# Two linear-attention layers on one core: norm scalars on GpSimd, sequence marks made once, a new instruction order

## The chip, the cores and the metric

The kernel runs on one core of a Trainium2 chip. The metric is the device time in microseconds (us) of one execution. A core has five engines with an in-order queue each: TensorE (PE; its weight loads are listed as PEld), VectorE (DVE), ScalarE (ACT), GpSimd (POOL) and SyncE (SP), which here issues all DMA transfers.

## What is computed

Input x has 32 sequences of 128 tokens with 512 features, all in float32. Two layers of the same build follow each other (layer 0 with 16 heads, layer 1 with 8). Cut to what matters, a layer is:

```
xn = layernorm(x) * w + b
q, k, v = xn @ Wq + bq, xn @ Wk + bk, xn @ Wv + bv      # 512 x 512 each
k, v masked at padded tokens
q = softmax(q over the features of a head); k = softmax(k over the tokens)
att = k^T v per head;  y = q att
scale, shift = split(silu(cond) @ We + be)              # cond: 32 x 1024
h = silu(layernorm(y) * (1 + scale) + shift) @ Wo + bo
x = x + h
```

In layer 0 the mask sets k to minus infinity. A sequence whose tokens are all masked therefore gives NaN in the reference, and the kernel carries this as a mark per sequence (`nanf`: 0, or NaN for a fully masked one) which is added to the residual stream in layer 1.

## The kernel before

**Jobs.** A job is two sequences (G = 2) of one layer; there are 16 jobs per layer, 32 in all, in one row. Tiles have 128 partitions. Per job: the rows of x are loaded (`z`), normalized, transposed to `xnT`, and multiplied with the weights. Products with the weights are done by a seven-product scheme (sums of blocks, `Sx` and `Sh`, made on GpSimd; sums of weights made once), in which each product lands in one of the PSUM banks `qa`, `qb`, `qc`, `qe`, `ka` and so on, and VectorE or ScalarE adds it to its destination (`kadd`, `qadd`, `oadd`). In the middle jobs (`far`) transposes are done by VectorE in 32x32 blocks plus DMA through DRAM (`zb`/`zd`, `k`/`kd`, `yb`/`yd`, and `qb` to `qT`); the first and the last job use PE transposes.

**Norm scalars.** `norm` takes the statistics of 512 features by `bn_stats` and `bn_aggr` on VectorE (`mv`: mean and variance), adds epsilon on VectorE (L570), raises to the power of -1/2 on GpSimd (L571, `rstd`), and makes -mean * rstd on VectorE (L573, `nmr`) for both sequences at once. ScalarE then normalizes with `nmr` as bias and `rstd` as scale (L585). The first and the last job (`apart`, also called edge) normalize on VectorE with mean and `rstd` directly (L581). There are two norms per job: "a" of x and "b" of y.

**Marks and residual.** In layer 0 every job makes the marks of its two sequences from its mask (L605 to L608: maximum over the masked row, comparison, reciprocal, product with zero), and GpSimd adds the output bias row to the residual tile `x` (L619). In layer 1 VectorE adds bias row and mark at once (L622). Then `oadd` adds the output products in quarters of 128x256 (L918), and the tile is stored.

**Order.** Nothing runs in program order. Every step is registered with `op(place, engine, cost, ...)` with a due time: the job's start (31 us per job) plus a due time written in the code plus a shift from the table `SHIFT[place]`. `Plan.schedule` then places the steps one by one by modelled costs, hops between engines (`HOP`, `SAFE`), buffers that come free, and due times. The emitted list fixes the order of each of the five queues, SP with its DMA issues among them. `lock=True` makes the planner keep VectorE and GpSimd steps apart. Before, the table has three stages: preparation, layer 0 and layer 1.

Of the kernel before, what the change touches and what calls it, by code (L numbers as in the profile page):

```python
# [38 lines left out]
    0: ([-3.7, -3.3, 10.9, -8.6, -4.2, 13.5, 4.9, 11.2, -18.2, 15.7], [-33.7, 9.7, -1.7, 28.5, -9.3], [14.4, 7.7]),  # L39
    1: ([], [-26.7], []),  # L40
    2: ([], [11.5], []),
    3: ([], [-31.7], []),
    4: ([], [-5.4], []),
    5: ([-16.7, -7, -12.1, -13.1, -3.6, -5.6, -16.5, -9.3, 22.1, -11.3, -17.4, 10.8], [], [-15.8, -20.2, 3.4, -3.6, -4.7, 13.7, 27, 5.9, 15.4, 2.5, -8.5, -11.3]),
    6: ([], [31.1, 22.7, 25.5, 1.5, 21.3, 20.6, -5.4, 18.5, 30.4, 28.7, 24.3, 22.4], [19.8, 18.9, 12.7, 41.8, 17.6, 19.7, 11.5, 33.5, 23, 31.2, 30.4, 14.8]),
    7: ([-32.7, -45.9, -34.3, -37.3], [-21, -27.4, -89.5, -25.3], [-16, -29.6, -16.3, -153.3]),
    8: ([-20.6, -23.4, 25.4, -50.1], [-20.3, -46.7, -5.3, -20.8], []),
    9: ([-33.4, -50.5], [-0.6, -8.9], []),
    10: ([16.7], [14.1], []),
    11: ([4.2], [48.6], []),  # L50
    12: ([5], [1.3], []),
    13: ([-18.6], [-4.2], []),
    14: ([-10], [14.9], []),
    15: ([19.1], [20.7], []),
    16: ([6.1], [], []),
    17: ([], [-103.2, -62, -106.9, -143.3, -159.3, -84.2, -88.8, -123.6], [-126, -130.5, -80.2, -30.5, 41.4, -77.8, -45.7, -9.4]),
    18: ([], [13.4, -27.4, -24.8], [-19.4, 46, -28.9]),
    19: ([], [-65.7, -82.4, -54.5, -91.8, -71.3, -58.9, -72.7, -62.7, -4.4, -61.3, -71.7, 1.2], [-88.4, -41.6, -56.9, -56.8, -67.7, -22.8, -22.6, -73.8, -126.4, -37.7, -117.1, -19]),
    20: ([], [49.4, 1.5, 71.9, 14.9], [77.1, -16.1, 62.3, -1.5]),
    21: ([], [58.9, 65, 31, 76.4], [78.7, 91.3, 57.5, 72.3]),  # L60
    22: ([], [66.3, -8, 5.7, -6.5], [-7.3, 50.9, 0.8, -8.9]),
    23: ([], [-23.5, 26.7, 58.4, 48.5], [-1.3, 58.3, 47.2, 35.9]),
    24: ([], [71.8, 1.1], [2.7, 30.5]),
    25: ([], [-16.9, -35.1, 13.9, -9.1], [5.1, 4.6, -17.3, -2.1]),
    26: ([], [65.9, 92.9, 20.2, -15], [1.2, 49.1, 24, 91.5]),
    27: ([], [-1.8], []),
    28: ([], [36.7], []),
    29: ([], [-70.3], []),
    30: ([], [-13.2], []),
    31: ([], [4.6], []),  # L70
    32: ([], [], [17]),
    33: ([], [-70.6, -36.8], []),
    34: ([], [], [20.7, 30]),
    35: ([], [-2.2, 52.4], [29.7, 43.1]),
    36: ([], [60.7, 29.9, 17.5, 35.6], [-22.4, -40.6, 16.5, 9.8]),
    37: ([], [0.9, -44.2], [-21.1, -40.5]),
    38: ([], [85.9, -9, 10.6, -29.4], [14.5, -6.6, 8.9, -45.6]),
    39: ([], [-50.7, -15, -36.2, -35.4, -53.2, -20, -62.5], [-45.9, -38.8, -4, 5.6, -15.3, -23.9, -141]),
    40: ([], [11.9, 18.7, 39.5, -35.9, -20.5, -34.5, 16.3, -33.4], [-27.7, -28.4, -11.5, -45.7, 20.4, -36.9, 6.6, -64.2]),
    41: ([], [-54.2, -47.2, -6.3, -19.6], [28.2, 8.8, -55.8, 21.1]),  # L80
    42: ([], [-47.8, -30.7, -46.4, -22.4], []),
    43: ([], [-24.9, -43, 11.6, 31.4], []),
    44: ([], [-54.4, -66.3], [-38.9, 25.9]),
    45: ([], [19.9, -42.6], [0.2, 2.4]),
    46: ([], [65.6, 73.3, 119, 122.5, 87.6, 49.7, 33.8, 82.8], [154.5, 165.3, 80, 165.8, 68, 49.2, 148.7, 120.9]),
    47: ([], [5.2, 0.8], [14.1, 37.1]),
    48: ([], [59.3, -10.4], []),
    49: ([], [-31.3, -4, -17.3, -29.4, -31.9, -35.8, -34.7], [-8, -9.4, -26.2, -33.6, -77.1, 5.2, -12.3]),
    50: ([], [-223, -129.1, -153.9, -150.7], [-149.5, -120.6, -102.4, -178.6]),
    51: ([], [-66.1, -38.1, -35, -81.1], [-64.5, -158.5, -51.3, -23]),  # L90
    52: ([], [-2.6, 1.4, 2.4, 16.2], []),
    53: ([], [5.4, -14.2, -29.9, -9.3], []),
    54: ([], [4.1, 24.4], [63.9, -18.5]),
    55: ([], [-51.7, -23.9], [-47.5, -89.4]),
    56: ([], [62.1, 69.2], [49.3, -25.6]),
    57: ([], [-18.1, -40.7], [-106.3, -28]),
    58: ([], [75.4, -28.7], [-7.9, -18.2]),
    59: ([], [83.4, 26.3], [29.1, 34.8]),
    60: ([], [55.2, 48.7, 115, 61, 38.4, 30, 73.5, 87, 1.5, -15.2, 72.4, -21.6, 21.2, 79.6, 85.8, 7.1], [45.5, 99.4, 58.5, 121.8, 14.6, 53.3, 3.3, 83.5, 17.6, 83.6, 152.4, 57.6, 10.2, 100, 99.7, 82.6]),
    61: ([], [53.1, 61.3], [45.3, 77.6]),  # L100
    62: ([], [-7.6, 11.1], [-3.7, 21.5]),
    63: ([], [-11.9, 26.1], [-9, 17.1]),
    64: ([], [76.4, 89.5], [85.6, 75.2]),
    65: ([], [-11, -1.1], [-16.2, 13]),
    66: ([], [], [21.8, -4.9]),
# [200 lines left out]
def act(n, pointers=0, psum=True):  # L306
    return (0.05 if psum else 0.093) + 0.093 * pointers + n / 1200
# [705 lines left out]
```

## Time and profile before

| what | us |
|---|---|
| runs shown, without profile | 932.77, 942.49, 942.39 (median 942.39) |
| the profiled execution, own time | 935.26 |
| its span, first to last instruction | 933.5 |
| PE busy | 906.3 (97%), 6292 matmuls |
| VectorE busy | 838.9 (90%) |
| ScalarE busy | 595.8 (64%) |
| GpSimd busy | 452.5 (48%) |
| DMA moved | 183.38 MB, mean 196 GB/s |
| granted TensorE clock, mean | 0.998 |

Busy times are unions of an engine's instructions. Ends of matmuls are modelled, so a busy PE is not PE at its peak; the distance of one row's start to the next tells more. The share of an engine is a mean over stages: the start, in which weights are loaded, the middle, in which two to three jobs overlap, and the end, in which the last job runs alone. A stage's idle time is its length less the busy time there. Groups of instructions are listed as: line, engine, operation, written tile <- read tiles, shape, count | busy us, mean ns of one | idle time before them, and what ended it.

### The profile page before, as it was taken

The page shows a single profiled execution, that of the slowest core. Times are in us where ns is not written, and L with a number is a line of the kernel's source. Part 1 is how long each engine was busy: PE and PEld are TensorE (multiplying, and loading weights), DVE is VectorE, ACT ScalarE, POOL GpSimd, SP SyncE. Part 2 cuts the span into 40 slices and gives each one's busy share as a digit, 9 for nine tenths or more (in the row PEclk, how much of TensorE's full clock was granted, in tenths as well). Part 3 has the DMA queues.
Part 4 walks back from the last instruction along what each step waited for, and adds up shares of the span by engine and source line. Part 5 has one row for each costly group of instructions (what it writes and reads, how often), then busy time and mean ns, then how long its engine had stood idle before and what let it go on. Part 6 is the DMA issues. An engine that isn't in the chain of part 4 may idle for free.

```text
span 933.5 us, 18771 instructions
## 1 busy us (share of the span) xinstructions
PE 906.3 (97%) x6292; PEld 637.8 (68%) x6292; DVE 838.9 (90%) x1844; ACT 595.8 (64%) x1503; POOL 452.5 (48%) x520
## 2 busy tenths in 40 slices
PE   6989999999999999999999999999999999999996
PEld 4546776676667667767766766777776767677675
DVE  5897989988789899799999999999989999888995
ACT  5447666585664957658577656766766756655652
POOL 3544475456554656556546344543444434343322
PEclk9999999999999999999999999999999999999999
DMA  9565568787676785778958876676767675655533
GB/s 324 179 195 156 163 186 229 206 259 206 189 211 201 188 237 156 204 225 236 274 165 226 229 230 169 184 220 187 196 203 214 209 202 144 172 158 140 155 121 109
DMA packets 239360, 183.38 MB, mean 196 GB/s; under 512 B 143136, under 2 KB 196896, under 8 KB 239264
## 3 DMA queue, kind: packets, MB, share of 16 engines
q1 hardware_dynamic: 239264, 182.18, 67.0%
q8 instruction: 50, 0.82, 0.4%
q14 instruction: 46, 0.38, 0.1%
HBM read 102.94 MB, written 63.44 MB: 178 GB/s over the span
## 4 chain that ended last, share of the span: by engine, by line
PE 55%; DVE 27%; DMA 7%; ACT 4%; SPq 4%; issue 2%; POOL 1%; ACTq 0%; DVEq 0%
PE bank_qa L739 10%; PE bank_qe L739 7%; PE bank_ka L665 5%; PE bank_oa L913 5%; PE bank_oe L913 4%; PE bank_qb L739 3%; PE bank_ke L665 3%; PE bank_py L868 3%; PE bank_qc L739 3%; DVE x L918 2%; PE bank_pa L847 2%; DMA yb<-yd 2%; PE bank_kb L665 2%; SPq L797 2%; PE bank_oc L913 2%
## 5 line engine op out<-in xcount | busy, mean ns | idle before, releaser
L710 POOL TENSOR_TENSOR kT<-kT,mb 128x512 f32<-128x512 f32 x64 | 82.7, 1297 | 107.3 <-DVE kT L676 80.8
L671 ACT ACTIVATE kT<-bank_ka,cols_c 128x128 f32<-128x128 f32 x248 | 75.2, 360 | 82.4 <-PE bank_ka L665 68.0
L717 ACT ACTIVATE kT<-kT,kmax 128x128 f32<-128x128 f32 x256 | 99.5, 390 | 37.4 <-DVE kmax L713 36.9
L739 PE MATMUL bank_qa<-wqv,Sx 128*128 128x512 f32 x248 | 117.5, 596 | 3.2 <-DVE v L743 2.0
L739 PE MATMUL bank_qe<-wqv,Sx 128*128 128x512 f32 x248 | 117.6, 596 | 1.7 <-DVE v L746 1.3
L899 ACT ACTIVATE hT<-yb,fc_c,fa_c 128x128 f32<-128x128 f32 x240 | 96.4, 481 | 9.2 <-DVE rstdb L570 8.8
L780 POOL TENSOR_TENSOR q<-q,qmax 128x512 f32<-128x512 f32 x64 | 67.6, 1065 | 62.1 <-DVE qmax L779 60.5
L544 POOL TENSOR_TENSOR Sx<-xnT 128x256 f32<-128x256 f32 x62 | 44.7, 737 | 98.8 <-PE bank_qe L739 71.0
L633 ACT ACTIVATE xnT<-zb,cols_c 128x256 f32<-128x256 f32 x116 | 60.8, 588 | 31.9 <-DMA zb<-zd 22.9
L585 ACT ACTIVATE y<-y,nmrb,rstdb 128x512 f32<-128x512 f32 x60 | 46.0, 805 | 44.8 <-DVE nmrb L573 44.7
L665 PEld LDWEIGHTS bank_ka<-Sx,wk 128*128 128x128 f32 x496 | 63.9, 192 | 15.2 <-issue 13.0
L739 PEld LDWEIGHTS bank_qe<-wqv,Sx 128*128 128x128 f32 x248 | 44.2, 190 | 41.2 <-issue 36.1
L665 PEld LDWEIGHTS bank_ke<-Sx,wk 128*128 128x128 f32 x496 | 62.9, 192 | 13.8 <-issue 9.3
L544 POOL TENSOR_TENSOR Sh<-hT 128x256 f32<-128x256 f32 x64 | 45.8, 728 | 52.7 <-ACT hT L899 50.0
L739 PEld LDWEIGHTS bank_qa<-wqv,Sx 128*128 128x128 f32 x248 | 43.7, 190 | 39.6 <-issue 33.6
L913 PE MATMUL bank_oa<-wo,Sh 128*128 128x256 f32 x256 | 66.6, 384 | 0.6 <-DVE x L918 0.2
L868 PEld LDWEIGHTS bank_py<-att_c,qT 128*128 128x128 f32 x512 | 61.1, 192 | 8.5 <-issue 4.3
L913 PE MATMUL bank_oe<-wo,Sh 128*128 128x256 f32 x256 | 65.8, 381 | 0.6 <-DVE x L918 0.5
L665 PE MATMUL bank_ke<-Sx,wk 128*128 128x128 f32 x496 | 65.7, 275 | 0.7 <-DVE kT L676 0.7
L665 PE MATMUL bank_ka<-Sx,wk 128*128 128x128 f32 x496 | 65.6, 275 | 0.0
L868 PE MATMUL bank_py<-att_c,qT 128*128 128x128 f32 x512 | 63.4, 276 | 2.0 <-DMA z<-in_x_dram 0.9
L585 ACT ACTIVATE z<-z,nmra,rstda 128x512 f32<-128x512 f32 x60 | 46.1, 805 | 28.8 <-DVE nmra L573 27.7
(126 smaller groups left out, 2225.6 us busy)
## 6 DMA issues: line engine op xcount, KB each, us to landing
x<-x SPq DMA_DIRECT2D x64, 256.0 KB, 3.7
kd<-k SPq DMA_DIRECT2D x30, 512.0 KB, 4.1
k<-kd SPq DMA_DIRECT2D x120, 128.0 KB, 3.2
qT<-qb SPq DMA_DIRECT2D x480, 32.0 KB, 2.3
yd<-yb SPq DMA_DIRECT2D x30, 512.0 KB, 3.5
yb<-yd SPq DMA_DIRECT2D x120, 128.0 KB, 3.4
zd<-zb SPq DMA_DIRECT2D x29, 512.0 KB, 3.2
zb<-zd SPq DMA_DIRECT2D x116, 128.0 KB, 3.4
```

What stands on the lines that cost most here:

```text
L544: op(17, "POOL", pool(2 * T), lambda i=i, x=x, y=y, f=f: nc.gpsimd.tensor_tensor(S.ap[:, i], x(), y(), f), r, [(S, i)], due=due, lock=True)
L585: op(26, "ACT", act(512, 2, False), lambda: nc.scalar.activation(dst.ap[:, b, :], src.ap[:, b, :], AF.Identity, bias=nmr.ap[:, b : b + 1], ...
L633: op(36, "ACT", act(GT, 2, False), lambda c=c: nc.scalar.activation(xnT.ap[:, c, :].rearrange("p (b r t) -> p r b t", b=G, r=4), zb.ap[:, ...
L665: nc.tensor.matmul(t.ap[:, m * T : (m + 1) * T], kw[quarter].ap[:, c, m * P : (m + 1) * P], a()[:, c, :], start=(first and m == 0 and c == ...
L671: op(40, "ACT", act(T, 1), lambda m=m: nc.scalar.activation(kT.ap[:, 2 * h + m, i, :], Ak.ap[:, m * T : (m + 1) * T], AF.Identity, bias=co ...
L710: op(44, "POOL", pool(2 * GT), lambda hs_=hs_: nc.gpsimd.tensor_tensor(kT.ap[:, hs_].rearrange("p m b t -> p m (b t)"), kT.ap[:, hs_].rear ...
L717: op(46, "ACT", act(T, 1, False) + 0.093, lambda m=m, b=b: nc.scalar.activation(kT.ap[:, m, b, :], kT.ap[:, m, b, :], AF.Exp, bias=km.ap[: ...
L739: nc.tensor.matmul(t.ap, a()[:, c, :], wqv[quarter].ap[:, c, :], start=(first and c == 0), stop=(c == 1), skip_group_check=not first)
L780: op(55, "POOL", pool(512, False), lambda qh=qh, qm=qm: nc.gpsimd.tensor_tensor(qh(), qh(), qm.ap[:, :H].unsqueeze(2).to_broadcast([P, H, ...
L868: nc.tensor.matmul(py.ap[:, m * P : (m + 1) * P], qTc(b, m), att.ap[:, b, m, :], start=True, stop=True)
L899: op(75, "ACT", act(T, 2, False), lambda c=c, b=b: nc.scalar.activation(hT.ap[:, c, b * T : (b + 1) * T].rearrange("p (r t) -> p r t", r=4 ...
L913: nc.tensor.matmul(t.ap[:, :hf], a()[:, c, :], ow[quarter].ap[:, c, :], start=(first and c == 0), stop=(c == 1), skip_group_check=not first)
```

## The change

- The epsilon add moves from VectorE to GpSimd, and so does the negated mean, which becomes two GpSimd instructions of one column each. A norm's scalars are then four GpSimd instructions in the middle jobs, in the first and last job two per sequence.
- The marks of all 32 sequences are made once: the transposed mask (128 tokens x 32 sequences) is loaded, turned into 0 or -1 by VectorE, summed over the tokens by a PE product with a tile of ones, and put through reciprocal and product with zero. The four VectorE instructions per job of layer 0 are gone.
- In layer 1 GpSimd now adds the bias row as in layer 0, and the mark is added with the first product of each output quarter (four of the eight adds per job become `scalar_tensor_tensor`).
- The order is made anew: the table has five stages (preparation, first job, rest of layer 0, layer 1, last job) with new shifts, and the planner's `SAFE` margins are other numbers.

```diff
-    SAFE = {"PE": 0.40, "DVE": 0.10, "ACT": 0.48, "POOL": 0.00, "SP": 4.34}
+    SAFE = {"PE": 0.49, "DVE": 0.20, "ACT": 0.00, "POOL": 0.36, "SP": 7.65}
...
-        stage = 0 if self.base < 0 else 1 + (self.base >= self.LAYER)
+        job = round(self.base / self.STEP)
+        stage = 0 if job < 0 else 1 if job == 0 else 2 if job < B // G else 3 if job < 2 * B // G - 1 else 4
...
+    k_yb = kind("yb", [P, 4, G, NC, 32], 2)
+    mT, ones, count = k_mi.new("T"), k_yb.new("ones"), bank.new("count")
+    load(mT, mask0T, part=lambda a: a[:, :B], due=8)
+    op(8, "POOL", 0.5, lambda: nc.gpsimd.memset(ones.ap[:, 0], 1.0), (), [ones], due=9)
+    op(9, "DVE", 0.15, lambda: nc.vector.tensor_scalar(nanf.ap, mT.ap[:, :B], 1.0, -1.0, ALU.is_equal, ALU.add), [mT], [nanf], due=9, lock=True)
+    op(10, "PE", mm(1, B), lambda: nc.tensor.matmul(
+        count.ap[:, :B], ones.ap[:, 0].rearrange("p b c t -> p (b c t)")[:, :P], nanf.ap, start=True, stop=True), [ones, nanf], [count], due=9)
+    op(11, "DVE", 0.15, lambda: nc.vector.reciprocal(nanf.ap, count.ap[:, :B]), [count], [nanf], due=9)
+    op(12, "DVE", 0.15, lambda: nc.vector.tensor_scalar(nanf.ap, nanf.ap, 0.0, None, ALU.mult), [nanf], [nanf], due=9, lock=True)
...
-            op(22, "DVE", 0.075, lambda b=b: nc.vector.tensor_scalar(rstd.ap[:, b], mv.ap[:, b, 1], EPS, None, ALU.add), [(mv, i) for _, i in key], key, due=due)
-            op(23, "POOL", 0.65, lambda b=b: nc.gpsimd.tensor_tensor(rstd.ap[:, b], rstd.ap[:, b], mhalf.ap[:, b], ALU.pow), [mhalf], key, due=due)
+            op(27, "POOL", 0.25, lambda b=b: nc.gpsimd.tensor_scalar(rstd.ap[:, b], mv.ap[:, b, 1], EPS, None, ALU.add), [(mv, i) for _, i in key], key, due=due)
+            op(28, "POOL", 0.65, lambda b=b: nc.gpsimd.tensor_tensor(rstd.ap[:, b], rstd.ap[:, b], mhalf.ap[:, b], ALU.pow), [mhalf], key, due=due)
             if not apart:
-                op(24, "DVE", 0.09, lambda b=b: nc.vector.scalar_tensor_tensor(
-                    nmr.ap[:, b], mv.ap[:, b, 0], -1.0, rstd.ap[:, b], ALU.mult, ALU.mult), key + [(mv, i) for _, i in key], [(nmr, i) for _, i in key], due=due)
+                for i in range(G):
+                    op(29, "POOL", 0.3, lambda i=i: nc.gpsimd.tensor_scalar(
+                        nmr.ap[:, i : i + 1], mv.ap[:, i, 0:1], rstd.ap[:, i : i + 1], -1.0, ALU.mult, ALU.mult), [(rstd, i), (mv, i)], [(nmr, i)], due=due)
...
-            op(28, "DVE", dve(256), lambda: nc.vector.tensor_reduce(some.ap, mb.ap.rearrange("p (b t) -> p b t", b=G), AX.X, ALU.max), [mb], [some], due=0)
-            op(29, "DVE", 0.1, lambda: nc.vector.tensor_scalar(some.ap, some.ap, 0.5 * NEG, None, ALU.is_ge), [some], [some], due=10)
-            op(30, "DVE", 0.12, lambda: nc.vector.reciprocal(some.ap, some.ap), [some], [some], due=10)
-            op(31, "DVE", 0.1, lambda: nc.vector.tensor_scalar(nanf.ap[:, b0 : b0 + G], some.ap, 0.0, None, ALU.mult), [some], [(nanf, j)], due=10)
...
-            if L == 0:
-                op(33, "POOL", pool(512), lambda b=b: nc.gpsimd.tensor_tensor(xg.ap[:, b, :], xg.ap[:, b, :], row(2), ALU.add),
-                   [rows_sb], [(xg, b)], due=20, lock=True)
-            else:
-                op(34, "DVE", 0.663, lambda b=b: nc.vector.scalar_tensor_tensor(
-                    xg.ap[:, b, :], xg.ap[:, b, :], nanf.ap[:, b0 + b : b0 + b + 1], row(2), ALU.add, ALU.add),
-                   [rows_sb, (nanf, j)], [(xg, b)], due=20, lock=True)
+            op(34, "POOL", pool(512), lambda b=b: nc.gpsimd.tensor_tensor(xg.ap[:, b, :], xg.ap[:, b, :], row(2), ALU.add),
+               [rows_sb], [(xg, b)], due=20, lock=True)
...
-        def oadd(i, h, t, due=37):
+        def oadd(i, h, t, first=False, due=37):
             s = slice(h * hf, (h + 1) * hf)
-            op(77, "DVE", dve(hf), lambda: nc.vector.tensor_tensor(xg.ap[:, i, s], xg.ap[:, i, s], t.ap[:, :hf], ALU.add),
-               [(xg, i), t], [(xg, (i, h))], due=due)
+            if first and L:
+                op(77, "DVE", 0.4, lambda: nc.vector.scalar_tensor_tensor(
+                    xg.ap[:, i, s], xg.ap[:, i, s], nanf.ap[:, b0 + i : b0 + i + 1], t.ap[:, :hf], ALU.add, ALU.add),
+                   [(xg, i), t, nanf], [(xg, (i, h))], due=due)
+            else:
+                op(78, "DVE", dve(hf), lambda: nc.vector.tensor_tensor(xg.ap[:, i, s], xg.ap[:, i, s], t.ap[:, :hf], ALU.add),
+                   [(xg, i), t], [(xg, (i, h))], due=due)
```

The whole table `SHIFT` is replaced as well (one line per place, three columns before and five after; the numbers are not shown).

## The prediction

> **What bounds the kernel now.** I read the page's part 1 first, then the heading of part 4, then a table of the span by stage, because a share over the whole span hides where time is lost.
>
> ```profile
> PE 906.3 (97%) x6292; PEld 637.8 (68%) x6292; DVE 838.9 (90%) x1844; ACT 595.8 (64%) x1503; POOL 452.5 (48%) x520
> PE 55%; DVE 27%; DMA 7%; ACT 4%; SPq 4%; issue 2%; POOL 1%; ACTq 0%; DVEq 0%
> ```
>
> The table of stages (per stage: its length, then busy time of each engine, then granted clock, DMA share, GB/s):
>
> ```profile
> 0.00:28.00 28.00, 19.43 (x84) 14.56 (x84) 15.70 (x34) 16.05 (x39) 10.35 (x19) 1.00 0.96 333
> 28.00:84.00 56.00, 53.23 (x310) 30.11 (x309) 49.53 (x108) 24.62 (x66) 26.77 (x26) 1.00 0.54 163
> 84.00:240.00 156.00, 155.46 (x1130) 108.19 (x1130) 138.97 (x321) 106.66 (x273) 87.13 (x100) 1.00 0.72 211
> 240.00:336.00 96.00, 92.06 (x643) 65.84 (x643) 87.06 (x193) 61.29 (x160) 54.83 (x62) 1.00 0.67 189
> 336.00:500.00 164.00, 162.52 (x1147) 113.50 (x1146) 154.17 (x339) 112.04 (x286) 92.34 (x102) 1.00 0.75 216
> 500.00:896.00 396.00, 394.55 (x2779) 281.58 (x2779) 369.17 (x795) 260.20 (x651) 170.68 (x199) 1.00 0.66 188
> 896.00:933.50 37.50, 29.08 (x209) 24.00 (x207) 24.33 (x58) 14.96 (x34) 10.41 (x15) 0.94 0.32 113
> ```
>
> Length less PE busy is PE's idle time: 8.6 + 2.8 in the start, 0.5 + 3.9 + 1.5 + 1.5 = 7.4 in the middle (84 to 896), 8.4 in the end; 27.2 us in all. In layer 1 (500 to 896) PE is idle 0.4% of the time: the timeline has job after job 27.33 us apart (the first product of qa at 655.76 and again at 683.09) with PE's rows end to end. So **TensorE is the bound**, and VectorE (93% in that stage) is the engine it would wait for. Of the 27.2 us, some 7.5 before the first product and 3.4 behind the last (adds and store) have to stay; about 16 us can be had at most.
>
> **The change, part by part.** Durations are means of groups with shapes kept apart.
>
> ```profile
> L619 POOL TENSOR_TENSOR x<-x,rows 128x512 f32<-128x512 f32 x32 | 40.6, 1287 | 2.3 <-DMA x<-in_x_dram 2.3
> L622 DVE SCALAR_TENSOR_TENSOR x<-x,nanf_c,we_rows 128x512 f32<-128x512 f32 x32 | 24.0, 759 | 0.2 <-DMA x<-x 0.2
> L571 POOL TENSOR_TENSOR rstdb<-rstdb,mhalf_c 128x2 f32<-128x2 f32 x30 | 21.4, 714 | 57.5 <-DVE rstdb L570 56.4 <-DVE nmra L573 0.3
> ```
>
> And from the views of single tiles (min/median/max in ns):
>
> ```profile
> L570 DVE TENSOR_SCALAR rstda<-mva x34: 145/169/1051, 4.1 to 767.1; 128x2 f32<-128x2 f32 x30, 128x1 f32<-128x1 f32 x4
> L573 DVE SCALAR_TENSOR_TENSOR nmrb<-mvb,rstdb x30: 140/158/1217, 103.9 to 902.1; 128x2 f32<-128x2 f32 x30
> L606 DVE TENSOR_SCALAR some<-some x16: 161/182/1275, 12.6 to 397.5; 128x2 f32<-128x2 f32 x16
>   DVE nmrb L573: 44.7, 21
> ```
>
> *Off VectorE.* The marks of layer 0 (L605 to L608): 6.5 + 7.2 + 2.5 + 5.9 = 22.1 us. The epsilon add (L570): 10.0 + 9.8 + 1.2 = 21.0. The negated mean (L573): 12.4 + 11.2 = 23.6. The residual add of layer 1 (L622): 24.0. Together 90.7. *Onto VectorE:* 64 first adds of layer 1 become three-input ones. On 512 columns three inputs take 759 against 680 for the two-input add of L743, so I take half of that, 40 ns, on 256 columns: 2.6 us; and three small ones for the marks, 0.5. VectorE goes to 838.9 - 87.6 = 751 us, 80%: 2.7 us less per job. Of this about 40 us is not arithmetic: these tiny instructions have a median of 160 to 180 ns and a maximum of 1.0 to 1.3 us, the length of a GpSimd add. The Trainium skill (SBUF — State Buffer, "Who interferes with whom") says that VectorE and GpSimd share a port pair under an exclusive lock, which a `tensor_scalar` or an instruction with two SBUF inputs takes. By the median alone the change frees about 50 us, by the means with this waiting 88. I take 88, because the first add of layer 1 now reads PSUM as its second tensor, which the rule leaves outside the lock, and the tiny instructions are gone. At 50, the middle's gain below is halved.
>
> *Onto GpSimd.* 68 epsilon adds and 120 negated means of one column. The trace has no such GpSimd row; the bounds are the 99 ns memset of 128x2 and the 579 ns power of 128x1, the nearest row is the one-input select of 128x128 at 292 ns. I take 250: 47 us (19 to 109). Plus 32 residual adds at 1287 ns: 41 us. GpSimd goes from 452 to 541 us, 58% (55 to 65%).
> A rule speaks against this: the Trainium skill (GPSIMD Engine Reference, "Engine selection") sends two-input elementwise work to VectorE, GpSimd being about 2 times slower. The rows agree (1287 against 759). By the rule the move costs 32 x 0.53 = 17 us; by the stage it costs nothing, since GpSimd is busy 43% of 500 to 896 and PE waits there for VectorE. If that cover went, the 17 us would appear. I take nothing.
>
> *The norm's chain.* Before: epsilon add on VectorE, power on GpSimd, negated mean on VectorE, two crossings, and each VectorE step queued behind others: in the job that begins at 655.76 the power of `rstda` ended at 660.02 and its negated mean began at 663.39. ACT waited 44.7 + 27.7 us for it. After: four GpSimd instructions, 0.25 + 0.71 + 2 x 0.25 = 1.5 us with small gaps, no crossing inside. In most places the new order has them one behind the other; in some a product with `ksum` that waits for ACT stands between the two negated means, and the norm then waits with it.
>
> *Marks once.* One load of the transposed mask, one memset, one 32-column product (0.1 us of PE). Layer 1 reads the result some 440 us later, so nothing waits. On SP the load stands behind `zd` and `z` loads of later jobs; the next mask load waits until VectorE has read it, with a `z` load, `zd` and `kd` queued behind it, whose data VectorE makes later anyway. Cost nothing; without that cover one transfer, about 4 us, once. On GpSimd three memsets (1.3 us) now precede the identity; the first statistics wait for x until 3.2 us, later than that.
>
> *Order anew.* All five queues differ, DMAs included; this can't be priced from the trace of before. Bounds: all removable idle gone, -16; or every middle stage as bad as 240 to 336 (4.1% idle, 33 us instead of 7.4), +26.
>
> **Sum.** *Start:* the second normalization of the first rows follows its power directly instead of one statistic later: PE's first product at about 7.6 instead of 8.3, -0.7; a third of the 2.8 us in 28 to 84, -0.9. *Middle:* two thirds of 7.4, -5; the rest is DMA, such as the 8.7 us load of We ahead of PE's 2.2 us stall at 252. *End:*
>
> ```profile
> 909.58 1.03 PE L913 MATMUL bank_oe<-wo,Sh 128*128 128x256 f32 x4
> 914.71 1.73 PE L888 MATMUL bank_htp<-ident_c,y 128*128 128x128 f32 x8 [4.09 <-DVE y L581]
> 915.00:920.00 5.00, 4.68 (x19) 3.42 (x18) 1.66 (x4) 4.33 (x13) 1.49 (x3) 0.66 0.33 107
> ```
>
> PE stands 4.1 us before the last transposes while VectorE does y, two residual adds of 0.7 each (L622, gone) and the statistics; then the granted clock is 0.66 for 5 us, 1.7 us lost. The new gap: 0.33 + 0.67 + 0.69 + 0.2 + 0.55 and a hop = 2.5 us, and about 0.4 more for the second half's power: -1.2. The Trainium skill (TensorE: Matmul & The Clock Gate, "Why this matters for your kernels") puts the limit for an idle gap at about 3 us: by it the whole 1.7 is saved, by the row alone nothing is known; I take half, -0.8. Sum: -1.6 - 5 - 2.0 = **-8.6**.
>
> The profiled execution took 935.26 (span 933.5): 926.7. Of the runs shown, one is 2.5 below it and two 7.1 above, so the median is 942.39; the same step from there is 933.8. A measurement of this kernel tells about 1% from no change.
>
> **Rivals.**
> *A, the forecast: 926.7, chance 0.55.* For it: PE's stalls name VectorE, which loses a tenth of its work.
> *B, hidden anyway: about 932, chance 0.30.* PE is at 99 to 100% in the middle, so the freed 88 us become VectorE idle time; only start and end gain, 3.6. For it: 0.4% idle in layer 1. Against: 3.9 us in 240 to 336, and the chain's 27% of VectorE.
> *C, the GpSimd queue: about 956, chance 0.11.* An instruction that waits for ACT or VectorE at the head of GpSimd's queue holds the norm's scalars behind it; ACT normalizes late, transposes and DMAs follow late, PE waits. Layer 0 is the place (GpSimd near 67%, two more adds and two products per job). At 0.4 us of PE per norm, 60 norms cost 24, less 3.6: +20. Slower begins at 0.14 us per norm (8.6 / 60). Against: GpSimd idles half of its time now, and jobs overlap, so that a late norm has other jobs' products to hide behind.
> *Other, 0.04:* the freed VectorE time goes into new waits for the port, gain halved.
>
> **Numbers.** Range 915 to 943: nearly all removable idle gone from the lowest run (933 - 16 is 917, with 2 for the spread), up to no gain on the higher runs. Faster by over 1%: most of A and a part of B, 0.56; within 1%: 0.33; slower: C, 0.11.
>
> **What would show it.** VectorE near 751 us and GpSimd near 541; no negated mean among what ACT waits for on VectorE; PE idle in the middle near 2.5 us; first product near 7.6; the last gap near 2.9 with full clock behind it. Wrong would be: PE idle over 10 us in the middle with rows that name GpSimd (C), or VectorE down and PE idle as before (B).

## The result, and the profile after

The changed kernel takes **933.82 us** (median of 21 runs, 929.3 to 940.23), the kernel before **937.95 us** beside it (21 runs, 932.77 to 944.97). The ratio is **0.9954, 95% interval 0.9934 to 0.9975**: 4.3 us faster, half of the 8.6 that were forecast. (The forecast's 933.8, stepped from the median of three runs, meets the 933.82 by luck: its base was 4.4 us too high and its step twice too large.) Both kernels spread by about 1% from run to run, and the profile shows one execution: that of before took 935.26, that of after 937.57, one low and one high in its own spread. Side by side the two pages show the changed kernel as the slower one. That has to be kept in mind with every line below; the sizes come from the ratios, the profiles say where things stand.

Part 1 of the page of after, and the table of stages (length, then busy time of each engine, granted clock, DMA share, GB/s):

```profile
PE 905.1 (97%) x6294; PEld 638.4 (68%) x6294; DVE 771.9 (83%) x1623; ACT 601.4 (64%) x1505; POOL 534.4 (57%) x741
```

```profile
0.00:28.00 28.00, 19.21 (x64) 13.23 (x64) 12.81 (x24) 14.39 (x32) 9.25 (x22) 1.00 0.93 317
28.00:84.00 56.00, 55.39 (x340) 34.75 (x338) 49.11 (x102) 29.84 (x83) 36.69 (x52) 1.00 0.57 166
84.00:240.00 156.00, 151.16 (x1129) 104.75 (x1129) 124.19 (x265) 101.86 (x262) 87.95 (x121) 1.00 0.76 209
240.00:336.00 96.00, 96.00 (x715) 67.94 (x714) 81.41 (x176) 65.64 (x167) 64.22 (x89) 1.00 0.77 213
336.00:500.00 164.00, 162.31 (x1086) 114.96 (x1085) 145.34 (x302) 110.47 (x277) 102.13 (x136) 1.00 0.76 205
500.00:896.00 396.00, 390.46 (x2783) 279.55 (x2783) 338.75 (x716) 263.87 (x661) 217.47 (x301) 1.00 0.67 189
896.00:935.60 39.60, 30.60 (x188) 23.20 (x186) 20.25 (x43) 15.34 (x31) 16.73 (x23) 0.90 0.28 95
```

Length less PE busy: PE's idle time in the middle (84 to 896) is 4.8 + 0 + 1.7 + 5.5 = 12.1 us, against 7.4 before; the end is 39.6 us against 37.5. The forecast named over 10 us there, in rows that name GpSimd, as a sign of C; of PE's waits in the middle GpSimd ends only 1.3 us, transfers 4.7. VectorE is down by 67 us and GpSimd up by 82. Some of the moved instructions, as groups with shapes kept apart (busy us, mean ns, then idle time of the engine before them):

```profile
L626 POOL TENSOR_TENSOR x<-x,we_rows 128x512 f32<-128x512 f32 x32 | 40.4, 1276 | 22.2 <-DMA x<-x 16.5 <-DMA k<-kd 4.9 <-DMA qT<-qb 0.6
L922 DVE SCALAR_TENSOR_TENSOR x<-x,nanf_c,bank_oa 128x256 f32<-128x256 f32 x48 | 22.6, 470 | 16.3 <-PE bank_oa L916 16.2
L586 POOL TENSOR_SCALAR nmrb<-mvb,rstdb 128x1 f32<-128x1 f32 x60 | 15.1, 266 | 2.9
L582 POOL TENSOR_SCALAR rstdb<-mvb 128x2 f32<-128x2 f32 x30 | 6.8, 225 | 57.2 <-DVE mvb L579 50.2 <-DVE mva L579 5.3 <-DVE ksum L723 0.2
```

A tiny instruction on GpSimd takes 225 to 266 ns (283 for nmra), as estimated. ACT's waits for the negated means are now waits on GpSimd (us in all, times, longest): 39.7 us where they were 72.4.

```profile
ACT y L598 <- POOL nmrb L586: 31.2, 18, 7.5
ACT z L598 <- POOL nmra L586: 8.5, 10, 2.0
```

### The profile page after: what moved, and what is told of

Read it like the earlier page. It is cut to its first block, busy times and chain, and to the rows that moved or that the text cites. A ratio compares the mean times of both kernels' runs of the same rounds, so it can differ in the third digit from the quotient of the medians.

```text
span 935.6 us, 18840 instructions
## 1 busy us (share of the span) xinstructions
PE 905.1 (97%) x6294; PEld 638.4 (68%) x6294; DVE 771.9 (83%) x1623; ACT 601.4 (64%) x1505; POOL 534.4 (57%) x741
## 5 line engine op out<-in xcount | busy, mean ns | idle before, releaser
L902 ACT ACTIVATE hT<-yb,fc_c,fa_c 128x128 f32<-128x128 f32 x240 | 98.3, 482 | 0.6 <-DMA yb<-yd 0.2
L871 PEld LDWEIGHTS bank_py<-att_c,qT 128*128 128x128 f32 x512 | 61.6, 192 | 14.6 <-issue 6.7
L785 ACT ACTIVATE q<-q 128x512 f32<-128x512 f32 x64 | 40.2, 628 | 35.5 <-POOL q L783 35.2
L556 POOL TENSOR_TENSOR Sx<-xnT 128x256 f32<-128x256 f32 x62 | 44.7, 736 | 26.6 <-ACT xnT L636 18.1
```

The costliest lines, as they stand in the source:

```text
L556: op(22, "POOL", pool(2 * T), lambda i=i, x=x, y=y, f=f: nc.gpsimd.tensor_tensor(S.ap[:, i], x(), y(), f), r, [(S, i)], due=due, lock=True)
L871: nc.tensor.matmul(py.ap[:, m * P : (m + 1) * P], qTc(b, m), att.ap[:, b, m, :], start=True, stop=True)
L902: op(75, "ACT", act(T, 2, False), lambda c=c, b=b: nc.scalar.activation(hT.ap[:, c, b * T : (b + 1) * T].rearrange("p (r t) -> p r t", r=4 ...
```

## What could explain a gain of half the forecast

- **T1**: TensorE sets the middle and VectorE's relief is hidden there (the forecast's B); the 4 us come from the new order.
- **T2**: relief pays, but GpSimd's added load gives part of it back (a mild form of C).
- **T3**: the moves gain what was forecast, and the new order doesn't add its share.

Most experiments freeze the order. In this kernel a planner sorts all instructions by planned time and then emits them, so an operation can keep its place and its planned cost while its last line issues it on another engine: the queues of the other engines stay instruction by instruction as they were. In the text below, us are differences of ratios times 937. With 95% confidence, a version against before is uncertain by 1.2 to 3.1 us, and one version against another (each was measured beside before) by 2.2 to 3.7 us. So differences of 2 or 3 us are at the edge of what can be told.

## Experiments: the moves apart from the order

**b_moves**: the order of before with all moves of the change.

```
- lambda b=b: nc.vector.tensor_scalar(rstd.ap[:, b], mv.ap[:, b, 1], EPS, None, ALU.add)
+ lambda b=b: nc.gpsimd.tensor_scalar(rstd.ap[:, b], mv.ap[:, b, 1], EPS, None, ALU.add)
- nc.vector.scalar_tensor_tensor(nmr.ap[:, b], mv.ap[:, b, 0], -1.0, rstd.ap[:, b], ALU.mult, ALU.mult)
+ [nc.gpsimd.tensor_scalar(nmr.ap[:, i:i+1], mv.ap[:, i, 0:1], rstd.ap[:, i:i+1], -1.0, ALU.mult, ALU.mult) for i in range(G)]
- nc.vector.scalar_tensor_tensor(xg.ap[:, b, :], xg.ap[:, b, :], nanf..., row(2), ALU.add, ALU.add)
+ nc.gpsimd.tensor_tensor(xg.ap[:, b, :], xg.ap[:, b, :], row(2), ALU.add)
- (the four operations of the mark chain)
+ j == 0 and nc.vector.memset(nanf.ap, 0.0)
- oadd(0, 0, Ao)                 (and three more first quarters)
+ oadd(0, 0, Ao, True)           (three inputs, as in the change)
```

> The order of the kernel before with all moves of the change in it: eps addition and nmr on GpSimd, layer 1's bias addition on GpSimd, three-input additions at the first output quarters, the per-job mark chain gone (left out: the marks themselves, nanf is set to zero). VectorE about 760, GpSimd about 540. T1: within 2 us of before, ratio 0.998 to 1.002, and the change's 4 us come from the new order. T2: no gain or slower, 0.998 to 1.006, ACT waits on nmr from GpSimd. T3 (the moves gain what was forecast and the new order gives it back at start and end): faster than the changed kernel, 0.988 to 0.993.

Measured: ratio **0.9946 (0.9925 to 0.9967)**, 5.1 us faster than before, with VectorE 773.4 and GpSimd 536.7. T1 falls: with the old order the moves give all of the gain. T3's stronger claim, that they would beat the changed kernel, isn't shown either: the two differ by 0.8 us, which is inside both intervals. So **the new order adds nothing that can be measured to what the moves give** (with it go the marks made once, which b_moves leaves out and which no run prices alone). T3 as it is put above, without that stronger claim, stays possible.

**a_all_dve**: the reverse, the changed kernel in its order with the moves (not the marks) undone. The negated mean stays two instructions of one column, where before has one of two.

```
- lambda b=b: nc.gpsimd.tensor_scalar(rstd.ap[:, b], ...)         + nc.vector.tensor_scalar
- lambda i=i: nc.gpsimd.tensor_scalar(nmr.ap[:, i : i + 1], ...)  + nc.vector.scalar_tensor_tensor
- nc.gpsimd.tensor_tensor(xg.ap[:, b, :], ..., row(2), ALU.add)   + (nc.vector if L else nc.gpsimd).tensor_tensor
```

> Every queue's order as in the changed kernel, but the eps addition, nmr and layer 1's bias addition are issued by VectorE again (marks stay as changed): VectorE about 772+75=845 us, GpSimd about 400. Changed kernel: 933.8 (0.9954 of before). T1 (TensorE sets the middle, VectorE's relief is hidden): within 2 us of the changed kernel, ratio to before 0.993 to 0.998. T2 (GpSimd's queue gives back what VectorE gains): as T1 or faster, because ACT's 40 us of waits on GpSimd's nmr go: 0.990 to 0.996. Forecast (the relief is what gains, 5 us in the middle): slower than the changed kernel by 4 to 8 us, ratio 0.999 to 1.004.

Measured: **0.9984 (0.9969 to 0.9998)**, 2.8 us slower than the changed kernel, VectorE 821.6, GpSimd 452.0. That is just outside T1's 2 us, but the interval reaches into it, and short of the forecast's 4 to 8; by itself this run settles little. New order and marks without the moves give 1.5 us (0.2 to 2.9).

**a_light**: is VectorE's relief still worth anything?

```
- nc.vector.bn_stats(st.ap[:, b, :], srcb.ap[:, b, :])
+ nc.vector.bn_stats(st.ap[:, b, :], srcb.ap[:, b, :64])
```

> Changed kernel with bn_stats over 64 of 512 columns (left out: the other columns' share in mean and variance): VectorE about 70 us less again (near 700), nothing put on GpSimd, same order and waits. T1: under 2 us faster than the changed kernel, ratio to before 0.993 to 0.997. T2: the moved norm scalars' waits stay, so the same as T1, but ACT's waits on GpSimd are not shorter. If VectorE still sets the middle (forecast): 0.985 to 0.990.

Measured: **0.9877 (0.9855 to 0.99)**, 7.2 us faster than the changed kernel for 50.8 us off VectorE (771.9 to 721.1): 0.14 us per us. VectorE at 83% of the span still sets the time in part. (The difference is uncertain by 2.9 us, the price by 0.06.) **b_light** is the same edit in the kernel before.

> The kernel before with bn_stats over 64 of 512 columns (left out: the other columns' share in mean and variance): VectorE about 51 us less than before (839 to 788), nothing put on GpSimd. The moves in before's order took 65 us off VectorE, put 84 on GpSimd and gave 5.0 us. If a microsecond off VectorE is worth the 0.14 us seen from the changed kernel to a_light, and GpSimd gave back the rest in the moves: 6 to 8 us faster than before, ratio 0.9915 to 0.9935. If GpSimd costs nothing and the first relief is worth less than later relief (5.0/65 = 0.08 each): 4 us, 0.995 to 0.9965.

Measured: **0.9928 (0.9902 to 0.9954)**, 6.7 us for 49.8 us off VectorE: 0.135 us per us. The page of b_light:

```profile
PE 906.7 (98%) x6292; PEld 640.0 (69%) x6292; DVE 789.1 (85%) x1844; ACT 595.7 (64%) x1503; POOL 456.7 (49%) x520
```

PE has the same work as before (906.3), and the span is 928.6 against 933.5: idle time went. The price is uncertain by 0.05. This price is that of pure relief, and an upper one, since shorter statistics also shorten each norm's chain. At 0.135 the 65.5 us that b_moves took off VectorE would be worth 8.8; they gave 5.1 (3.1 to 7.0). That points to T2, but a price 0.05 lower would explain it too.

## Experiments: what GpSimd's load costs

**a_pool_light** and **b_pool_light** take load off GpSimd and change no instruction of VectorE.

```
- qh(), qh(), qm.ap[:, :H].unsqueeze(2).to_broadcast([P, H, dh]), ALU.subtract
+ qh()[:, :H//4], qh()[:, :H//4], qm.ap[:, :H//4].unsqueeze(2).to_broadcast([P, H//4, dh]), ALU.subtract
```

> The changed kernel with GpSimd's subtraction of qmax over a quarter of the heads (left out: the subtraction for the other heads): GpSimd about 45 us less (534 to 490), VectorE the same. If GpSimd's longer queue gives back part of the gain (ACT's 40 us of waits on nmr from GpSimd): 2 to 4 us faster than the changed kernel, ratio to before 0.991 to 0.9935. If GpSimd's load is free: as the changed kernel, 0.9945 to 0.9965.

> The kernel before with GpSimd's subtraction of qmax over a quarter of the heads (left out: the subtraction for the other heads), as in a_pool_light: GpSimd about 40 us less, VectorE the same. If GpSimd's load costs 0.04 to 0.07 us per us: 1.6 to 2.8 us faster than before, 0.997 to 0.9985. If only the changed kernel's longer GpSimd queue hurts (a_pool_light's 2.7 us): 0.999 to 1.001.

Measured: a_pool_light **0.9926 (0.9903 to 0.9949)**, 2.6 us faster than the changed kernel for 39.4 us off GpSimd; the two intervals overlap, so alone it settles nothing. b_pool_light **0.9968 (0.9951 to 0.9984)**, 3.0 us faster than before for 39.5 us, clear of no change. That is 0.076 us per us at most, since the shorter subtraction also shortens the chain of q, and VectorE's busy time fell by 5.6 us with the same instructions (838.9 to 833.3). It was not the changed kernel's queue alone that was short of time: a GpSimd busy 48% of the span already costs.

**b_dup** puts the load on without relief: VectorE works as before, and GpSimd repeats the moved work into places that nobody reads.

```
+ nc.gpsimd.tensor_scalar(st.ap[:, b, 0], mv.ap[:, b, 1], EPS, None, ALU.add)                     (beside each eps addition)
+ nc.gpsimd.tensor_scalar(st.ap[:, i, 1:2], mv.ap[:, i, 0:1], rstd.ap[:, i:i+1], -1.0, ...) for i (beside each nmr)
+ j > 1 and nc.gpsimd.tensor_tensor(R[0].ap[:, 0, :], row(2), row(1), ALU.add)                    (beside each bias addition)
```

> The kernel before, VectorE's work unchanged, with GpSimd doing the moved work as well, into places nobody reads: the eps addition and nmr of every norm, and in layer 1 (from its third job on) a 128x512 addition for each bias addition. GpSimd about 80 us more (452 to 532), as after the change; nothing waits for these results. If GpSimd's load by itself gives back 3 to 4 of the 8.5 us that 65 us off VectorE are worth at b_light's price: 3 to 4 us slower than before, ratio 1.003 to 1.0045. If the load is free, and the price of relief is smaller in the moves for another reason: 0.999 to 1.001.

Measured: **1.0156 (1.0134 to 1.0179)**, 14.6 us slower, four times what was expected. The groups say why (L625 issues both):

```profile
L625 POOL TENSOR_TENSOR rows<-we_rows 128x512 f32<-128x512 f32 x28 | 38.2, 1365 | 0.4
L625 DVE SCALAR_TENSOR_TENSOR x<-x,nanf_c,we_rows 128x512 f32<-128x512 f32 x32 | 33.5, 1058 | 0.0
```

VectorE's bias addition takes 1058 ns where it took 759, and 785 in the next experiment, which leaves the copy out: the copy stands beside it in time, and both read two tensors from SBUF. The experiment built a collision that the change doesn't have. PE's idle time in 500 to 896 rose from 1.45 to 10.3 us, while in layer 0 (84 to 500), where only the scalars were copied, it stayed (6.0 to 4.3). **b_dup_norm** leaves the copies of the bias addition out.

> As b_dup, but without its copies of the bias addition: VectorE as before, GpSimd does the eps addition and nmr of every norm as well, into places nobody reads (about 41 us more, 452 to 495). In b_dup the copy of the bias addition stood beside VectorE's own and stretched it from 759 to 1058 ns, and the time was lost in layer 1 alone. If the small scalars' load on GpSimd is cheap and b_dup's 14 us were that collision: 0.999 to 1.001. If GpSimd's load costs 0.05 us per us whatever it is: 1.002 to 1.003. If most of b_dup's loss was the scalars: over 1.006.

Measured: **1.002 (1.0005 to 1.0034)**, 1.9 us slower for 47.3 us of load: 0.04 us per us (0.01 to 0.07; for b_pool_light 0.04 to 0.12). So GpSimd's load costs by itself, also where nobody waits for its result: this part of T2 is shown, in the order of before. For the 84.2 us of b_moves the two prices make 3.4 to 6.4 us given back, and 8.8 less that is 2.4 to 5.4; measured 5.1. With such wide prices this agrees, but proves no size.

What the load delays can be seen in part. A copy stands in GpSimd's queue ahead of results that VectorE needs, so VectorE waits for these: in all 12.3 to 15.0 us for GpSimd in three kernels with the order and the middle of before (before, b_tail, b_tail_fit), 20.8 in b_dup_norm, 19.1 in b_moves. One such wait, before and in b_dup_norm:

```profile
DVE nmrb L573 <- POOL rstdb L571: 2.2, 4, 0.8
DVE nmrb L576 <- POOL rstdb L572: 7.1, 9, 1.5
```

How these waits reach PE isn't shown.

## Experiments: which of the moves pays

**b_norm_pool** makes only the first two edits of b_moves, **b_bias_marks** only the others.

> The kernel before, in its order, with only the eps addition and nmr issued by GpSimd: VectorE about 28 us less, GpSimd about 41 more. By the price of pure relief (0.13 us per us of VectorE, from b_light) 3.7 us faster, ratio 0.996. If the norm scalars' longer way through GpSimd's queue gives it back (T2): 0.999 to 1.003, and ACT's waits on nmr grow to 80 us as in b_moves.

> The kernel before, in its order, with only layer 1's bias addition on GpSimd, the three-input additions at the first output quarters and no mark chains (left out: the marks, nanf is zero): VectorE about 37 us less, GpSimd about 42 more. By the price of pure relief 4.8 us faster, 0.995. T2 (GpSimd's cost sits in the norm scalars, which others wait for, not in the bias, which nobody waits for): all of the 5 us that b_moves gave, 0.993 to 0.996. If GpSimd's load itself costs, whatever it is: half, 0.997 to 0.999.

Measured: b_norm_pool **0.9982 (0.9969 to 0.9996)**, 1.7 us; b_bias_marks **0.9955 (0.994 to 0.997)**, 4.2 us. They add up to 5.9, against 5.1 for both. In the old order the bias and the marks pay most. The norm scalars' 34.3 us off VectorE (4.6 at the price) and 50.7 us on GpSimd (2.0 to 3.9) leave 0.7 to 2.6: measured 1.7. For b_bias_marks, whose profiled execution shows only 26.7 us off VectorE, prices explain 2.1 us at most; why it gave twice that is open (at the far ends of the prices' intervals it could be chance). In both b_norm_pool and b_moves ACT's waits for the negated means grew, from 72.4 us to 84.4 and 85.0.

**a_norm_dve** and **a_bias_dve** undo one of them in the new order (lines as in a_all_dve).

> The changed kernel, in its order, with only the eps addition and nmr back on VectorE: VectorE about 800, GpSimd about 493. By the price of pure relief 3.7 us slower than the changed kernel, 0.9995. T2 (moving the norm scalars gains nothing): as the changed kernel, 0.9935 to 0.997.

> The changed kernel, in its order, with only layer 1's bias addition back on VectorE: VectorE about 21 us more, GpSimd about 41 less. By the price of relief alone (0.13) 2.8 us slower than the changed kernel, 0.998. If the 41 us off GpSimd give 2 us back: 0.996 to 0.9975. a_norm_dve lost 3.9 us and a_all_dve, which is both, 2.8, so the bias may even be worth the other sign in this order: 0.9935 to 0.995.

Measured: a_norm_dve **0.9996 (0.998 to 1.0012)**, 3.9 us slower than the changed kernel; a_bias_dve **0.9973 (0.996 to 0.9985)**, 1.8 us slower. Here the norm scalars seem to pay most, and T2 in the form in which it was put for a_norm_dve (the scalars gain nothing) is refuted in this order. The two sum to 5.7 where both at once cost 2.8; each difference is uncertain by about 2.4, so that the bias in this order isn't clear of no gain. Nor are the pairs quite alike: b_bias_marks also takes off the marks and adds the three-input additions, which a_bias_dve leaves as they are. Each part gave between 1.7 and 4.2 us; that the scalars pay more in the new order fits what ACT waits for the negated means there: 39.7 us with them on GpSimd, 57.3 with them on VectorE (a_norm_dve), where the old order has it the other way round.

## Experiments: the ends

**a_tail** fills PE's bubbles in the last job with products that nobody reads, so that the clock may stay up.

```
+ if edge and L and b: warm(py, 10)     (behind the last job's second py)
+ if edge and L and b: warm(tp, 5)      (behind its last transposes)
  warm: for _ in range(count): nc.tensor.matmul(t.ap[:, :256], w.ap[:, 0, :P], w.ap[:, 1, :], start=True, stop=True)
```

> Changed kernel with 10 idle products (128x256, 2.2 us) between the last job's output products of attention and its last transposes, and 5 (1.1 us) behind these; nothing reads them. If the clock gate's 6.8 us at half speed behind 914 us follow from TensorE standing almost empty from 909 to 915, the drop goes or falls to 3.4 us: 1.7 to 3.4 us faster than the changed kernel, ratio to before 0.992 to 0.9935. If the clock drop has another cause, or the end waits on VectorE, ACT and GpSimd: no change or up to 1 us slower, 0.995 to 0.997.

Measured: **0.9908 (0.9878 to 0.9938)**, 930.13 us, 4.3 us faster than the changed kernel and the fastest version that leaves nothing out. PE's timeline at the end of after (start, duration, what; in brackets the idle time before it and who ended it), then its table in steps of 3.41 us, then the same work in a_tail (`warm` in a name cut off by the view is the filling), which begins some 7 us earlier:

```profile
908.37 1.05 PE L871 MATMUL bank_py<-att_c,qT 128*128 128x128 f32 x8
911.59 0.66 PE L891 MATMUL bank_htp<-ident_c,y 128*128 128x128 f32 x4 [2.16 <-DVE y L594]
912.91 0.66 PE L891 MATMUL bank_htp<-ident_c,y 128*128 128x128 f32 x4 [0.67 <-DVE y L594]
914.81 2.08 PE L916 MATMUL bank_oc<-wo,hT 128*128 128x256 f32 x4 [1.24 <-ACT hT L894]
916.68 3.62 PE L916 MATMUL bank_oa<-wo,hT 128*128 128x256 f32 x8
```

```profile
907.25:910.66 3.41, 2.18 (x15) 1.82 (x13) 3.28 (x8) 1.73 (x3) 0.81 (x2) 1.00 0.35 130
910.66:914.08 3.42, 1.31 (x8) 0.84 (x8) 1.38 (x4) 1.75 (x6) 1.00 (x2) 1.00 0.54 155
914.08:917.49 3.41, 2.68 (x6) 2.19 (x7) 0.00 (x0) 3.41 (x10) 0.85 (x2) 0.50 0.07 26
917.49:920.90 3.41, 3.41 (x9) 2.70 (x8) 0.48 (x1) 0.57 (x2) 3.25 (x5) 0.50 0.00 0
```

```profile
900.30 4.48 PE L607 MATMUL ank_warmbank_py<-wo 128*128 128x256 f32 x20
904.62 1.04 PE L901 MATMUL bank_htp<-ident_c,y 128*128 128x128 f32 x8
905.49 2.32 PE L607 MATMUL nk_warmbank_htp<-wo 128*128 128x256 f32 x10
907.65 1.03 PE L928 MATMUL bank_oc<-wo,hT 128*128 128x256 f32 x4
908.52 1.89 PE L928 MATMUL bank_oa<-wo,hT 128*128 128x256 f32 x8
```

In after the first group of oc takes 2.08 us and oa's eight 3.62; in a_tail 1.03 and 1.89. The records of the granted clock show after at half speed from 914.08 to 920.90. Every run lists its mean granted clock; span times (1 - clock) is the time lost to it: **3.4 to 3.8 us on average before, 4.7 after, 0.3 in a_tail**. Its products were too many, though: from start to start 10 took 4.3 us where the bubble was 2.2, and all 15 took 6.5 where the three bubbles add up to 4.1. So 3.4 us of PE time won at full clock were in part spent again. In the traces the end itself (from the start of the last py product to the end of the span) is 27.2 us in after and 25.9 in a_tail, 1.3 shorter. Of the 4.3 us (uncertain by 3.4) only so much is seen there; ahead of it the two kernels have the same instructions in the same order.

**a_tail_half** has 5 and 2.

> The changed kernel with 5 and 2 idle products in its last job in place of a_tail's 10 and 5. In a_tail one took 0.43 us, so 10 took 4.3 us where the gap was 2.3 and 5 took 2.2 where it was 1.2: about 3 us of the last job was spent on them. If 2.2 and 0.9 us are enough to hold the clock at full speed: 2 to 3 us faster than a_tail, ratio to before 0.988 to 0.9895. If they are too few and the clock drops for one step of 3.4 us: as a_tail, 0.990 to 0.992.

Measured: **0.9909 (0.9876 to 0.9943)**, as a_tail. In its trace, at full clock, the end takes 24.6 us, 1.3 less than in a_tail; in some of its runs the clock still drops (1.1 us lost on average), which may be what takes that back. Six runs can't tell.

**b_tail** and **b_tail_fit** do it in the kernel before, with 10 and 5 and with 8 and 1.

> The kernel before with the same 15 idle products in its last job (10 ahead of the last transposes, 5 behind them), all else in its order. Before's records show a mean clock of 0.9964 over 27 runs, which is 3.4 us of TensorE work lost at half speed, the changed kernel's 0.9950 4.7 us. If the clock's loss is a cost of the end that both kernels have, and the changed one only a little more of it: clock 0.999 or more and 3 to 4 us faster than before, ratio 0.9955 to 0.997. If only the new order's end suffers from it: ratio 0.998 to 1.001.

> The kernel before with 8 and 1 idle products in its last job in place of b_tail's 10 and 5: 8 take 3.4 us where before's gap is 4.1, where b_tail's took 4.3 and 2.2 us and gave back what the clock gained. If before's end loses its 3.4 us to the clock alone: 2.5 to 3.5 us faster than before, ratio 0.996 to 0.9975, clock 0.999. If the end is set by the chain through VectorE, GpSimd and ACT: within 1 us of before, 0.999 to 1.001.

Measured: **0.9989 (0.9975 to 1.0003)** and **0.999 (0.9973 to 1.0007)**, about 1 us. The clock's loss fell to 0.6 and 0.8 us, and yet 2 us of it weren't gained. In b_tail the filling itself takes 6.5 us, more than the bubbles; in b_tail_fit it fits, and its trace says what took the rest. The last transposes follow the product oe by 5.13 us in both kernels, behind VectorE's y; then ACT's hT sets when the output products go on, before first and b_tail_fit second:

```profile
918.46 1.20 PE L913 MATMUL bank_oa<-wo,hT 128*128 128x256 f32 x4 [0.32 <-ACT hT L891]
926.54 1.13 PE L925 MATMUL bank_oa<-wo,hT 128*128 128x256 f32 x4 [0.60 <-ACT hT L903]
```

This is 3.75 and 3.83 us behind the transposes. From oe to the last product the end takes 20.4 us in both. The slow clock of before lay in time in which PE would have waited for VectorE and ACT anyway, so its loss (span times the missing clock) wasn't time of the kernel. So what a clock kept up is worth depends on what is behind it in the order.

**a_ends** is a_tail with 11 filling products on the tile of ones ahead of the first transposes and 4 behind each of the first two.

> The changed kernel with idle products at both ends: 15 in the last job as before in a_tail, and 19 of 128x256 at the start (11 ahead of the first transposes, on the tile of ones that is ready at 1 us, 4 behind each of the first two), so that the clock is full when the first k products come at 11 us. If the slow clock until 16.4 us eats the head start of the new order: the k products (24 in 8.1 us) take 5.5 us, 1.5 to 3 us faster than a_tail, ratio to before 0.9875 to 0.9895. If the start is set by the weights' transfers (DMA share 0.93 of the first 28 us): as a_tail, 0.990 to 0.9915.

Measured: **0.9946 (0.993 to 0.9961)**, 3.6 us slower than a_tail. The record of a full clock begins at 6.5 us (after: 16.4; the tables show the time ahead of the first record as 1.00), and the first k products took 5.2 us instead of 8.1, but started at 12.9 instead of 11.0 behind the fillings, which I had sized at half of their cost. The next transposes came at 18.1 us, against 17.8 in a_tail: nothing gained at the start. What made it 3.6 us slower (uncertain by 3.2) isn't shown. Its clock also dropped once in the middle, at 211 us (below).

## Why the forecast was wrong

Two steps of the forecast failed. It put GpSimd's added load at nothing, where runs show that load alone costs (0.04 to 0.08 us per us, 3.4 to 6.4 us for the moves); and it put start and end at -3.6, where the new order gave nothing that can be measured (+0.8, uncertain by 2.8). The first is why the moves gave 5.1 us and not the 8.8 of their relief, as far as the prices can be trusted; the second is what is missing in the forecast's own sum. The two splits are not the same: the forecast goes by stage, the experiments by moves and order, and what the moves did at the ends is in the 5.1.

*The bound: right.* PE is busy 97% in both, and VectorE is what it waits for in part.

*Off VectorE, "87.6 us": mis-sized.* The durations of its rows do sum to 87.3 less (951.0 to 863.7), but its busy time fell by 67.1. The 20 us are overlap: a row begins before the one ahead has ended. In the timeline of VectorE before (start, duration):

```profile
664.50 0.45 DVE L573 SCALAR_TENSOR_TENSOR nmrb<-mvb,rstdb 128x2 f32<-128x2 f32 x1
664.88 0.41 DVE L676 TENSOR_TENSOR kT<-kT,bank_ke 128x256 f32<-128x256 f32 x1
665.21 0.67 DVE L779 TENSOR_REDUCE qmax<-q 128x8 f32<-128x512 f32 x1
```

The three last 1.53 us in sum and occupy 1.38. Means times counts over-count by some 0.08 us for each of these overlaps; the change took away 221 instructions of VectorE. The Trainium skill (Perfetto Trace Analysis, "Optimizing Scalar/DVE Operations") says as much: a profiled instruction overlaps with the next one by about its access overhead, some 60 ns on SBUF. By that figure 221 instructions make 13 us, an estimate of 74 us off VectorE; the trace has more overlap. The mean (88) was too high. The median pricing was mis-summed: the medians give 57 us and not 50, and the waiting is 31 us and not 40 (an estimate from the rows of rstd, nmr and some). The three-input addition costs 64 ns more than the two-input one (470 against 406), where I took 40.

*Onto GpSimd, "541": right (534.4), but "I take nothing" for it was wrong.* The argument was that GpSimd is idle half of the time and that PE waits for VectorE. b_pool_light and b_dup_norm put 0.04 to 0.08 us on each microsecond of load, 3.4 to 6.4 us in all. C had the right engine, a cost far too large (20 us, from 0.4 us per norm) and a path that holds only in part: ACT's waits for the norms grew in the old order (72.4 to 85.0) and shrank in the new one (39.7), and in b_dup_norm the added waits are VectorE's. The 17 us that the engine-selection rule would charge for the bias didn't appear either: b_bias_marks shows it gaining together with the marks, and a_bias_dve shows no loss from it.

*The middle, "-5": right in sum, not by its working.* The moves gave 5.1 us over the whole kernel, as the balance of about 9 gained and 4 given back, not as two thirds of PE's 7.4 us of idle; that the number fits is luck. That the profile of after shows 12.1 us there says little: a_tail has the same instructions in the same order up to the last job, and its middle has 6.0 (its four rows of 84 to 896: 153.47, 96.00, 163.02, 393.49 busy of 156, 96, 164, 396). Of the 6.1 us between them 2.1 are waits for single late transfers (4.7 against 2.6); most of the rest are waits for VectorE (2.7 against 0.5) and ACT (3.2 against 2.0).

*The start, "-1.6": not shown.* PE's idle time in the first 84 us fell from 11.3 to 9.4, but PE also ran longer at the slow clock. The first product came at 6.17, earlier than the 7.6 forecast, but PE then waited 1.5 us for the second z, and the clock became full at 16.4 us instead of 14.1. The q products that follow began at 21.10 against 21.28: the head start was gone.

*The end, "-2.0": the wrong sign.* The gap ahead of the last transposes did shrink from 4.09 to 2.16, better than the 2.9 forecast. But it came back in two smaller ones, 0.67 and 1.24, with little PE work between them, and the clock stayed down for 6.8 us instead of 3.4. From 896 on PE's idle time went from 8.4 to 9.0 us, the loss to the clock from 1.7 to 3.4. Shortening the longest gap isn't what keeps the clock. This is not the new order's doing alone: the traces of b_moves and b_bias_marks, in the old order, also have 6.8 us. With filling the end was 1.3 (a_tail) and 2.7 us (a_tail_half) shorter in the traces.

*The base.* The forecast was made from one profiled execution (935.26), with three runs of before at hand that had a median of 942.39; 21 give 937.95. Its chances were split at 1%, and the change moved the time by 0.46%.

So the sum reads: forecast -1.6 - 5 - 2.0; shown, moves -5.1, new order +0.8 with an uncertainty of 2.8, in which the clock's loss is 0.9 to 1.3 us larger than in before and 1.6 larger than in b_moves (3.1).

## What to carry to other kernels

An engine that is not the bound is not free: near the bound both engines have a price per microsecond, here about 0.14 for VectorE at 83 to 90% and 0.04 to 0.08 for GpSimd at half, and a move between them is worth the difference. (Each price is uncertain by a third or more.) Measure that price once, by making a frequent instruction cheaper in place and in order, before costing moves at full or at nothing. Where engines' rows are read as costs, take busy time, not the sum of durations, and at a ragged end count PE's work in the clock's window, not its longest gap.

## What the hardware showed that was not expected

The granted clock changes only at whole steps of 3.413 us from where it first becomes full. Before: full at 14.10, down 901.119 us later (264 steps); after: 897.705 (263). It falls after one step with little work and comes back after one or two. The Trainium skill (TensorE: Matmul & The Clock Gate, "Part 1: The HAM clock gate (the "warmup" mystery)") has that window; but the limit of about 3 us for a gap that it gives under "Why this matters for your kernels", from which the forecast took half of a saving, doesn't hold here. In the step of after ahead of the drop (910.66 in the table under a_tail) PE was busy for 1.31 of 3.42 us and no gap was longer than 2.16; after the step before that, with 2.18 busy, the clock stayed.

The 19 traces of this case, cut into these steps, agree on PE's busy time in a step as the measure. At full clock every step with up to 1.46 us (b_bias_marks, the first line below) was followed by the drop, and none of the some 5000 with more than 1.76 (b_tail_fit, the second line); between these bounds some kept it, the lowest with 1.51 (b_tail, from 930.13).

```profile
248.55:251.97 3.42, 1.46 (x10) 1.17 (x10) 3.42 (x7) 1.00 (x2) 1.96 (x2) 1.00 0.14 23
239.53:242.94 3.41, 1.76 (x11) 1.17 (x10) 0.58 (x2) 3.38 (x9) 0.59 (x2) 1.00 1.03 261
```

At half clock it came back after every step with at least 2.93 us (b_moves, from 237.38) and after none with up to 2.75 (a_norm_dve, from 919.39). That is why after, with 2.68 us in its first slow step, lost a second one. PE's ends are modelled, so these bounds are as the profile counts.

The clock makes single late transfers dearer: in a_ends the product of y waited for one, the clock fell at 211.32 us (60 steps) and stayed at half for 3.4 us. After had a shorter stall at the same instruction (1.83 us) and kept its clock.

```profile
211.74 3.11 PE L890 MATMUL bank_py<-att_c,qT 128*128 128x128 f32 x13 [2.52 <-DMA yb<-yd]
```

That is part of why the same kernel differs by 1% from run to run, but not the larger part: in the five sets of runs of before, time and loss to the clock go together with a correlation of 0.34 to 0.48, so the loss goes with an eighth to a quarter of the variance.
